# Graph-network kernel on one core: the order of work in the first batch element, and which queue loads the biases

## The chip, the cores and the metric

The kernel runs on one core of a Trainium2 chip. A core has TensorE (PE in the profile, with its weight loads as PEld), VectorE (DVE), ScalarE (ACT), GpSimd (POOL) and SyncE (SP); DMAs are issued here by SP and by POOL. The metric is the device time of one execution in microseconds (us); less is better. The time of the kernel before is a median of 3 runs.

## The reference, cut to what matters

There are 16 batch elements of 1024 nodes with 128 features, each with a dense 1024x1024 adjacency matrix `adj`, all in float32. A first graph layer and then a network of four layers are applied, each followed by a residual and a layer norm:

```python
degree = adj.sum(-1)
sum_neighbors = einsum('bid,bij->bjd', x, adj) / degree
x = layernorm(x + relu(concat([x, sum_neighbors]) @ W.T + b))

# four times, on fpass = x, later on concatenations with earlier layers' features
src_agg = einsum('bjv,bij->biv', nodes @ ws + bs, adj / row_norms)
dst_agg = einsum('bjv,bji->biv', nodes @ wd + bd, adj / column_norms)
fpass = tanh(concat([src_agg, nodes @ wn + bn, dst_agg]) @ wu + bu)

x = layernorm(x + fpass)
```

The kernel multiplies each layer's `ws`, `wd`, `wn` by the parts of `wu` beforehand ("folding"), and the row and column norms are sums of squares of `adj`, raised to the power -0.5.

## The kernel before, in words

The 16 elements go one after the other. While element b runs its four layers, element b + 1 is loaded and its first layer, norms and factors are prepared in the shadow of b's matmuls. Element 0 has nobody ahead of it, so lines 1131 to 1461 are an order written out by hand: each line of Python puts one instruction at the end of one engine's queue, and an engine works through its queue in order. "Hooks" hang work of the other engines at a numbered step of a layer's matmuls. Only this opening, and helpers it calls, are touched.

- **Loads.** `adj[0]` comes as four pairs of row blocks (`load_pair`, L1138), each pair half by SP and half by POOL. Block i = h*4 + k; the pairs come in the order 4-5, 6-7, 0-1, 2-3. After the pairs SP issues the broadcast bias `b0r` (L1198), the weights of layers 0 and 1 (L1200), two of the eight DMAs of row quarter 2, the nine small bias rows of set 0 (`load_biases`, L1163), the rest of row quarter 2, then bias set 1, layer 2's weights, bias set 2, layer 3's weights, and the row quarters 3, 0 and 1 (`load_rows`, L669). The row quarters are a second copy of `adj[0]`, read row-wise, which is scaled by ACT (`scale_rows`, L684) and transposed by DVE (`transpose_rows`, L690) into `at`.
- **First layer.** PE accumulates `x` times each block into `pa` (`gather`, L1242), two halves per block. `to_xT` (L1179) transposes x, `into_rows("px", ...)` (L1264) multiplies it by half of W, `gathered` (L1271) copies `pa` out, `into_rows("pg", ...)` multiplies that by the other half. DVE adds the bias (`x_and_bias`, L1274), the second product (`with_degrees`, L1277), the residual (`with_x`, L1283) and takes the norm's statistics (`two_stats`, L1287), whose powers POOL computes (L1301, L1303); `written` (L1305) writes the normed rows, one of them by ACT with `norm_write_act`. `to_x1` (L1310) transposes them for layer 0's messages.
- **Squares.** ACT squares each block; POOL sums the squares into `sq[4]` (`add_square`, L1232), while DVE adds `sq[7]` to `sq[6]` (L1322), `sq[2]` to `sq[1]` (L1341, names `first` = 2, `second` = 3) and finally `sq[3]` to the sum (L1404). `root_inverses` (L395) gives the row factors by a power on POOL; `inverses` (L382) does the same for the columns from PE's `pc`.
- **Folding.** `bias_columns` (L1169) transposes a set of biases on PE; `fold_begin` (L200) and `fold_end` (L224) make the folded weights of a layer on PE and copy them out on ACT. `fold_end` of layer 2 does its two chunks together, after `to_x1(0)` (L1407).
- **Layer 0 of element 0** (`plain_layer`, L889): 34 steps of one matmul each (two passes in the profile): 2 of own weights (`z`), 8 and 8 of `d` on the unscaled `a`, 16 of `z` on `at`. Its hooks are at L1456: `weights0` (sums of layer 2's weights, nine DVE instructions) at step 0, the column `inverses` at 2, the transposes of row quarters 2 and 3 at 3, `cinv0` (column factors into a row, PE and ACT) at 6, scaling of quarter 0 at 8, `second0` at 11 (DVE multiplies four tiles by `cinv`), `fold_last` at 13 (layer 3's folding, then scaling of quarter 1), four such multiplications on POOL at 14 (L1459), and so on. `finish(0)` after the last step and ACT's tanh (L1107) release the last messages of layer 1.

Of the kernel before, what the change touches and what calls it, by code (L numbers as in the profile page):

```python
# [23 lines left out]
def adj_resnorm_kernel(ctx: ExitStack, tc: tile.TileContext, x, adj, w0, b0, layers, out):  # L24
# [33 lines left out]
    nc = tc.nc  # L58
# [162 lines left out]

        return biases if later else biases()

    def fold_end(l, fetched):  # L224
        _, wur, _, wm, wTs = fetched
        for c in range(CHUNKS[l]):
            pm = small(f"wm{l}_{c}", [HW]) if c < 2 else product(f"wm{l}_{c}")
            for k in range(3):
                nc.tensor.matmul(pm[:, k * P:(k + 1) * P], wTs[c][:, k], wur[:, PART[k]],
                                 start=True, stop=True)  # L230
            nc.scalar.copy(message_weights_of(wm, l, c), pm[:, :2 * P].rearrange("p (a v c) -> p a v c", a=2, v=2))
            nc.scalar.copy(own_weights(wm, l, c), pm[:, 2 * P:3 * P])
        if l not in PAIRED:
            nc.sync.dma_start(wsave[l], wm.rearrange("p c v -> p (c v)")[:, :WIDTH[l]])
        elif l == 3:
            nc.sync.dma_start(wsave[l], wm)
# [923 lines left out]
    columns = [raw.take(len(v)) for v in biases_of]  # L1160
    bcs = [columns[0][:, 1:5], columns[0][:, 5:], columns[1], columns[2]]

    def load_biases(i, q):  # L1163
        for k, v in enumerate(biases_of[i]):
            q.dma_start(in_rows[k:k + 1, i * P:(i + 1) * P], v.rearrange("(o p) -> o p", o=1))

    b0r = one.tile([P, N], F32, tag="acc", name="b0r")[:, :P]
# [28 lines left out]
    places[1] = one.tile([P, 2 * NJ, HW // 2], F32, tag="T2", name="rows1_0")  # L1196
    rows, fetched = {}, []
    nc.sync.dma_start(b0r, b0.rearrange("(o p) -> o p", o=1).to_broadcast([P, P]))  # L1198
    for l in (0, 1):
        fetched.append(fetch_weights(raw, l, nc.sync, bcs[l], None if l else wm))  # L1200
    load_rows_piece(0, 2, places[2], 0, QB, (0,))
    load_biases(0, nc.sync)
    rows[2] = [load_rows_piece(0, 2, places[2], 0, QB, (1, 2, 3))]
    for l in (2, 3):
        load_biases(l - 1, nc.sync)
        fetched.append(fetch_weights(raw, l, nc.sync, bcs[l]))
    wm = as_chunks(wm, 0)
    for q in (3, 0, 1):
        rows[q] = load_rows(0, q, [places[q]])

    nc.vector.memset(mhalf, -0.5)
# [20 lines left out]
    def add_square(i):  # L1232
        nc.gpsimd.tensor_add(sq[4], sq[4], sq[i])
# [8 lines left out]
    def gather(h, i):  # L1242
        nc.tensor.matmul(pa[h], xn[:, i], a[:, i, half(h)], start=(i == BPH), stop=(i == BPH - 1))
# [3 lines left out]
            square(i)  # L1247
            degree(i)

    def gathers_of(h, k):  # L1250
        for i in range(h * BPH + k, h * BPH + k + 2):
            for h2 in (1, 0):
                gather(h2, i)

    agT = one.tile([P, N], F32, tag="f1T", name="agT0")
    xw = one.tile([P, NB, D], F32, tag="f23T", name="xw0")
# [60 lines left out]
    squares_of(*PAIRS[0])  # L1317
    gathers_of(*PAIRS[0])
    squares_of(*PAIRS[1])
    gathers_of(*PAIRS[1])  # L1320
    to_xT(0)
    nc.vector.tensor_add(sq[6], sq[6], sq[7])  # L1322
    add_square(5)
    add_square(6)
    degree_inverses(1)
    squares_of(*PAIRS[2])
    gathers_of(*PAIRS[2])
    add_square(0)
    first, second = 2, 3
    nc.scalar.activation(sq[second], a[:, second, :], AF.Copy, accum_out=cols[:, 2 * NB + second:2 * NB + second + 1])  # L1330
    degree(first)
# [2 lines left out]
    square(first)  # L1334
    degree_inverses(0)
    x_and_bias(1)
    gathered(1)
    into_rows("px", xT, 0, 0)
    into_rows("pg", agT, 1, 1)
    square(second)  # L1340
    nc.vector.tensor_add(sq[1], sq[1], sq[first])  # L1341
    add_square(1)
    x_and_bias(0)
    gather(0, first)
    bias_columns(0)
    gather(0, second)
    gathered(0)
# [4 lines left out]
    into_rows("pg", agT, 1, 0)  # L1352
    two_stats(1, 2)
    root_inverses(cols, inv, slice(NB))
    biases()
    fold_end(0, fetched[0])
    with_degrees(0, range(2))
    written(1, 0, norm_write_act)
    biases = fold_begin(1, fetched[1], later=True)
    for q in range(1, BPH):  # L1360
        written(1, q)
    with_degrees(0, range(2, BPH))
    spread = row_inverses(0, inv)
    to_x1(1)
    biases()
# [1 line left out]
    with_x(0)  # L1367
    two_stats(0, 0)
    two_stats(0, 2)
    for q in range(BPH):  # L1370
        written(0, q)

# [11 lines left out]
    for b in range(B):  # L1384
# [7 lines left out]
        f1 = feature(b, "f1T")  # L1392
        if b == 0:
            def row_factors0():
                scale_rows(rows[2], 2, rinv, range(2, QB))
                scale_rows(rows[3], 3, rinv)

            def second_x1():
                nonlocal rinv
                bias_columns(1)  # L1400
                fold_begin(2, fetched[2])
                rinv = gather_inverses(0, spread)
                scale_rows(rows[2], 2, rinv, range(2))
                nc.vector.tensor_add(sq[4], sq[4], sq[second])  # L1404
                ahead["tr"] = column_transpose(0, st0)

            def factors_and_fold():  # L1407
                to_x1(0)
                fold_end(2, fetched[2])
                column_reduce(0, st0, ahead["tr"])  # L1410

            ahead = {}
            t = messages(b, 0, feats, wm, {0: second_x1, 1: factors_and_fold, 2: row_factors0}, with_sums=False)
            cinv = {}

            def columns0(rows, h, engine=nc.vector):
                scale_columns(a, cinv[0], rows, half(h), engine)

            def weights0(destination, finish):
                sums_of_weights(2, fetched[2][3])  # L1420
                weight_sums(own_seven(2, fetched[2][3]))
                nc.sync.dma_start(wsave[2], fetched[2][3])

            def rows0(destination, finish):
                for q in (2, 3):
                    transpose_rows(rows[q], q, at)

            def cinv0(destination, finish):
                cinv[0] = factor_rows_now(0, 1, inv, "cinv")

            def second0(destination, finish):
                columns0(range(NJ, NB), 1)
                destination(1, cinv[0])

            def first_rows(destination, finish):
                for q in (0, 1):
                    transpose_rows(rows[q], q, at)
                columns0(range(NJ), 1)

            def fold_last(destination, finish):  # L1440
                bias_columns(2)
                fold_begin(3, fetched[3])
                scale_rows(rows[1], 1, rinv)

            def first0(destination, finish):
                destination(0, cinv[0])
                columns0(range(NJ), 0)

            def sums0(destination, finish):
                combine_1(y)  # L1450
                combine(2, y, T)
                finish(1)
                combine_1(yt)
                combine(3, y, T)

            hooks = {0: weights0, 2: lambda *_: inverses(0, st0, NB), 3: rows0, 6: cinv0,  # L1456
                     8: lambda *_: scale_rows(rows[0], 0, rinv), 
                     11: second0, 13: fold_last, 15: first_rows, 16: lambda *_: fold_end(3, fetched[3]),
                     14: lambda *_: columns0(range(NJ, NB), 0, nc.gpsimd), 18: first0, 26: sums0}  # L1459
            T = combined(0, "T")  # L1460
            plain_layer(b, 0, feats, t, wm, a, at, f1, "acc", hooks)
            wm = message_weights(b, 1)
            a2 = load(n)
            xs2 = load_spread(n)
        else:
            w = {}
            if nxt:
                st = begin_sums(n)
            t = messages(b, 0, feats, wm)
            if nxt:  # L1470
                w["a"] = load(n)
            Q = combined(b, "Q")
            ahead = {}

            def weights1(ahead=ahead):
                combine(4, y, T)
                ahead["wm"] = message_weights(b, 1)

            def rows3():
                transpose_rows(rows[0], 0, at)  # L1480

            def sums1(w=w, st=st):
                if nxt:
                    for i in range(2):
                        squares_of_row(n, w["a"], st, i)

            def additions(*which, then=(), w=w, st=st):
                def issue():
                    if nxt:
                        for i in which:  # L1490
                            add_squares(n, st, i)
                        for i in then:
                            squares_of_row(n, w["a"], st, i)
                return issue

            hooks = {0: rows3, 3: weights1, 5: lambda: combine_1(yt), 7: lambda: combine(2, yt, Q),
                     9: lambda: combine(3, yt, Q), 15: sums1, 16: additions(1), 17: lambda: combine(4, yt, Q),
                     18: additions(then=(2, 3)), 23: additions(2), 27: additions(3)}
            aggregate(b, 0, feats, t, wm, a, at, T, Q, f1, "row", hooks)
            wm = ahead["wm"]  # L1500
            a2, xs2 = w.get("a"), None
# [343 lines left out]
```

## Time and profile before

| | |
|---|---|
| median of 3 runs | 2378.79 us (2378.77 to 2379.21) |
| the profiled execution | 2379.08 us |
| its span, first to last instruction | 2377.3 us, so 1.8 us lie around it |
| PE busy | 2364.5 us, 99% |
| DVE busy | 2094.0 us, 88% |
| ACT busy | 980.7 us, 41% |
| POOL busy | 274.1 us, 12% |
| granted TensorE clock, mean | 0.998 |

One execution is shown. In a timeline row the columns are start and duration in us, engine, line and operation, out<-in with the shapes, how many were merged, and in brackets the idle time before it and what ended that. A line such as L249 is that of a helper and serves several layers. A row with xN runs from the first one's start to the last one's end. Time in this text counts from the span's start.

### The profile page before, as it was taken

How to read it: one execution, taken by the hardware profiler on the slowest of the kernel's cores; microseconds unless marked ns; L12 is line 12 of the kernel's file. 1: busy time of each engine (PE TensorE's matmuls, PEld its weight loads, DVE VectorE, ACT ScalarE, POOL GpSimd, SP SyncE). 2: the span in 40 equal slices, each digit the busy share in tenths (PEclk: the TensorE clock that was granted, in tenths of full speed). 3: DMA queues.
4: the chain of work that ended last, by engine and by line, in shares of the span. 5: the costliest groups of instructions: out<-in, count | busy, mean ns of one | idle time of the engine just before them, and what ended most of it. 6: DMA issues, size and time to landing. Idle time of an engine off the chain costs nothing.

```text
span 2377.3 us, 39282 instructions
## 1 busy us (share of the span) xinstructions
PE 2364.5 (99%) x15268; PEld 1323.0 (56%) x15268; DVE 2094.0 (88%) x2835; ACT 980.7 (41%) x1858; POOL 274.1 (12%) x102
## 2 busy tenths in 40 slices
PE   8999999999999999999999999999999999999998
PEld 5455555555555555555655555555555555555555
DVE  7999998998989989889988889898899998998954
ACT  5425334352443524445243452534425334352322
POOL 4000111101111011110011110111100111101100
PEclk9999999999999999999999999999999999999999
DMA  9537263362634527244273442635436263362400
GB/s 208 126 87 148 58 136 76 79 142 49 153 66 95 119 52 168 51 104 108 63 156 68 98 97 72 151 67 119 84 76 146 58 139 75 80 140 49 100 22 22
DMA packets 363548, 232.10 MB, mean 98 GB/s; under 512 B 150385, under 2 KB 334466, under 8 KB 363362
## 3 DMA queue, kind: packets, MB, share of 16 engines
q1 hardware_dynamic: 360722, 226.24, 42.9%
q0 software_dynamic: 816, 2.49, 0.4%
q8 instruction: 121, 1.98, 0.4%
q10 hardware_dynamic: 1824, 0.85, 0.1%
q14 instruction: 65, 0.53, 0.1%
HBM read 209.66 MB, written 19.84 MB: 97 GB/s over the span
## 4 chain that ended last, share of the span: by engine, by line
PE 96%; DMA 2%; DVE 1%; SPq 0%; ACT 0%; issue 0%; POOLq 0%; POOL 0%; DVEq 0%
PE m L1094 43%; PE z L1094 26%; PE pt L249 9%; PE pt_z L249 5%; PE m_f L624 5%; PE z_f L624 3%; PE pw L249 2%; PE m3s L1094 2%; DMA Q<-in_adj_dram 1%; PE pt_p L249 1%; DMA b0r<-in_L_gnn_b_dram 1%; SPq L681 0%; DMA a<-in_adj_dram 0%; DVE a L436 0%; DMA wsave<-wm 0%
## 5 line engine op out<-in xcount | busy, mean ns | idle before, releaser
L1094 PE MATMUL m<-a,t 128*64 128x512 f32 x1008 | 426.8, 593 | 0.0
L1094 PE MATMUL m<-at,t 128*64 128x512 f32 x1008 | 420.4, 592 | 0.0
L1094 PE MATMUL m<-T,S 128*64 128x512 f32 (+1 forms) x1040 | 398.6, 572 | 0.0
L1094 PE MATMUL m<-Q,S 128*64 128x512 f32 x880 | 392.3, 592 | 0.0
L484 POOL TENSOR_TENSOR rs<-ve,mhalf 128x32 f32<-128x32 f32 x30 | 191.6, 6387 | 1019.3 <-DVE ve L482 1019.3
L1094 PE MATMUL z<-at,t 128*64 128x512 f32 (+1 forms) x520 | 229.6, 579 | 0.0
L1094 PE MATMUL z<-a,S 128*64 128x512 f32 x504 | 228.3, 592 | 0.0
L1094 PE MATMUL z<-Q,t 128*64 128x512 f32 (+1 forms) x520 | 227.5, 580 | 0.0
L1094 PE MATMUL z<-a,t 128*64 128x512 f32 (+1 forms) x520 | 227.4, 580 | 0.0
L1094 PE MATMUL z<-at,S 128*64 128x512 f32 x504 | 226.6, 592 | 0.0
L1094 PEld LDWEIGHTS m<-Q,S 128*64 128x64 f32 x880 | 119.4, 137 | 185.1 <-issue 184.8
L1094 PEld LDWEIGHTS m<-T,S 128*64 128x64 f32 x1040 | 133.4, 137 | 122.6 <-issue 117.5
L1094 PEld LDWEIGHTS m<-at,t 128*64 128x64 f32 x1008 | 133.6, 137 | 113.7 <-issue 113.7
L1094 PEld LDWEIGHTS m<-a,t 128*64 128x64 f32 x1008 | 131.5, 137 | 97.5 <-issue 92.8
L946 ACT COPY e<-m 64x512 f32<-64x512 f32 x63 | 36.6, 582 | 338.9 <-PE m L1094 338.5
L1094 PE MATMUL z<-T,t 128*64 128x512 f32 (+2 forms) x400 | 173.0, 575 | 0.0
L397 POOL TENSOR_TENSOR inv<-cols,mhalf 128x16 f32<-128x16 f32 (+1 forms) x16 | 49.6, 3102 | 937.7 <-DVE cols L396 937.7
L436 DVE TENSOR_TENSOR a<-a,cinv 128x512 f32<-128x512 f32 x252 | 153.1, 681 | 0.0
L324 ACT ACTIVATE sq<-a 128x1024 f32<-128x1024 f32 x120 | 125.8, 1050 | 32.7 <-DVE acc L331 18.8
L1094 PEld LDWEIGHTS z<-Q,t 128*64 128x64 f32 x520 | 69.6, 137 | 106.0 <-issue 105.7
L249 PEld LDWEIGHTS pt<-wm,f1T 128*64 128x64 f32 x1536 | 112.0, 137 | 26.7 <-issue 14.7
L319 ACT ACTIVATE a<-a 128x1024 f32<-128x1024 f32 x120 | 125.3, 1045 | 0.4
(329 smaller groups left out, 4997.6 us busy)
## 6 DMA issues: line engine op xcount, KB each, us to landing
a<-in_adj_dram SPq DMA_DIRECT2D x120, 512.0 KB
rows<-in_adj_dram SPq DMA_DIRECT2D x480, 64.0 KB
a<-in_adj_dram SPq DMA_DIRECT2D x240, 128.0 KB
wm<-wsave SPq DMA_DIRECT2D x32, 704.0 KB
wm<-wsave SPq DMA_DIRECT2D x31, 320.0 KB
xs<-in_x_dram SPq DMA_DIRECT2D x60, 128.0 KB
cinv<-dr SPq DMA_DIRECT2D x30, 256.0 KB
dinv<-dr SPq DMA_DIRECT2D x30, 256.0 KB
```

The source lines that it names most:

```text
L249: nc.tensor.matmul(out[s], x[:, s], y, start=start, stop=stop)
L319: nc.scalar.activation(a[:, i, :], a[:, i, :], AF.Copy, accum_out=degree)
L324: nc.scalar.activation(sq, a[:, i, :], AF.Square, accum_out=state["cols"][:, i:i + 1])
L397: nc.gpsimd.tensor_tensor(inv[:, s], cols[:, s], mhalf[:, s], ALU.pow)
L436: engine.tensor_mul(a[:, i, s], a[:, i, s], cinv[:, s])
L484: nc.gpsimd.tensor_tensor(rstd, ve, mhalf[:, :n], ALU.pow)
L624: nc.tensor.matmul(o, x_, y_, start=start, stop=stop)
L946: nc.scalar.copy(e0[high], A[high])
L1094: nc.tensor.matmul(o, x, y_, start=start, stop=stop)
```

## The change

It reorders the opening and moves some DMAs. SP loads five of the nine biases of set 0 straight after `b0r`, then the weights of layers 0, 1 and 2, then row quarters 2, 3 and 0, then layer 3's weights, then quarter 1. POOL's queue loads the other biases between its additions of squares. `to_xT(0)` goes between the two gathers of the second pair, and x's products `px` of half 0 before the third pair. `gather(0, first)` goes ahead of `pg` of half 1. The DVE addition of `sq[2]` to `sq[1]` is dropped: POOL adds `sq[1]` and, after `root_inverses`, `sq[2]` by itself. Row 0 of half 1 is written by ACT ahead of layer 0's folding copies. `fold_end` of layer 2 is split around `to_x1(0)`. All eight rows of quarter 2 are scaled in one place. The column inverses come at step 4, the weight sums at 5, the transposes at 6, `cinv0` at 8, and quarter 0's scaling at 9.

```diff
-    def fold_end(l, fetched):
+    def fold_end(l, fetched, chunks=None):
         _, wur, _, wm, wTs = fetched
-        for c in range(CHUNKS[l]):
+        for c in range(CHUNKS[l]) if chunks is None else chunks:
...
-    def load_biases(i, q):
-        for k, v in enumerate(biases_of[i]):
+    def load_biases(i, q, s=slice(None)):
+        for k, v in list(enumerate(biases_of[i]))[s]:
...
-    for l in (0, 1):
+    load_biases(0, nc.sync, slice(0, 5))
+    for l in (0, 1, 2):
         fetched.append(fetch_weights(raw, l, nc.sync, bcs[l], None if l else wm))
-    load_rows_piece(0, 2, places[2], 0, QB, (0,))
-    load_biases(0, nc.sync)
-    rows[2] = [load_rows_piece(0, 2, places[2], 0, QB, (1, 2, 3))]
-    for l in (2, 3):
-        load_biases(l - 1, nc.sync)
-        fetched.append(fetch_weights(raw, l, nc.sync, bcs[l]))
     wm = as_chunks(wm, 0)
-    for q in (3, 0, 1):
+    for q in (2, 3, 0, 1):
+        if q == 1:
+            fetched.append(fetch_weights(raw, 3, nc.sync, bcs[3]))
         rows[q] = load_rows(0, q, [places[q]])
...
-    def gathers_of(h, k):
+    def gathers_of(h, k, between=None):
         for i in range(h * BPH + k, h * BPH + k + 2):
             for h2 in (1, 0):
                 gather(h2, i)
+            if between is not None and i == h * BPH + k:
+                between()
...
-    gathers_of(*PAIRS[1])
-    to_xT(0)
+    gathers_of(*PAIRS[1], lambda: to_xT(0))
     nc.vector.tensor_add(sq[6], sq[6], sq[7])
     add_square(5)
+    load_biases(0, nc.gpsimd, slice(5, 7))
     add_square(6)
+    load_biases(0, nc.gpsimd, slice(7, 8))
     degree_inverses(1)
+    into_rows("px", xT, 0, 0)
     squares_of(*PAIRS[2])
     gathers_of(*PAIRS[2])
     add_square(0)
+    load_biases(0, nc.gpsimd, slice(8, 9))
+    add_square(1)
+    load_biases(1, nc.gpsimd)
...
     x_and_bias(1)
+    x_and_bias(0)
     gathered(1)
-    into_rows("px", xT, 0, 0)
+    gather(0, first)
     into_rows("pg", agT, 1, 1)
     square(second)
-    nc.vector.tensor_add(sq[1], sq[1], sq[first])
-    add_square(1)
-    x_and_bias(0)
-    gather(0, first)
     bias_columns(0)
     gather(0, second)
...
     root_inverses(cols, inv, slice(NB))
+    add_square(first)
     biases()
+    written(1, 0, norm_write_act)
     fold_end(0, fetched[0])
-    with_degrees(0, range(2))
-    written(1, 0, norm_write_act)
     biases = fold_begin(1, fetched[1], later=True)
     for q in range(1, BPH):
         written(1, q)
-    with_degrees(0, range(2, BPH))
+    with_degrees(0, range(BPH))
...
     two_stats(0, 2)
+    load_biases(2, nc.gpsimd)
...
-                scale_rows(rows[2], 2, rinv, range(2, QB))
+                scale_rows(rows[2], 2, rinv)
...
-                scale_rows(rows[2], 2, rinv, range(2))
...
             def factors_and_fold():
+                fold_end(2, fetched[2], (0,))
                 to_x1(0)
-                fold_end(2, fetched[2])
+                fold_end(2, fetched[2], (1,))
...
-            hooks = {0: weights0, 2: lambda *_: inverses(0, st0, NB), 3: rows0, 6: cinv0,
-                     8: lambda *_: scale_rows(rows[0], 0, rinv), 
+            hooks = {4: lambda *_: inverses(0, st0, NB), 5: weights0, 6: rows0, 8: cinv0,
+                     9: lambda *_: scale_rows(rows[0], 0, rinv), 
```

## The prediction

> **What bounds the kernel now.** I read the waits of PE first, then PE's, DVE's and POOL's timelines up to 90 us. PE is busy 99% of the span. These are all of its waits:
>
> ```profile
> PE pa L1243 <- DMA a<-in_adj_dram: 2.0, 1, 2.0
> PE idle L1187 <- DVE mhalf L1211: 1.5, 1, 1.5
> PE biases L1172 <- DMA biases<-in_L_gnn_bu_dram: 0.8, 1, 0.8
> PE px L1269 <- ACT w0T L1192: 0.7, 1, 0.7
> PE bm L211 <- DMA raw<-in_L_gnn_wu_dram: 0.7, 1, 0.7
> PE pt L249 <- ACT f1T L1107: 0.6, 1, 0.6
> PE on L1762 <- DVE f23T L1757: 0.3, 1, 0.3
> PE bm L211 <- ACT wm L232: 0.3, 1, 0.3
> ```
>
> After 80.61 us (the wait for f1T) PE never waits again until 2365 us. So the change moves the end by as much as it moves PE at 80.61. Its matmuls stay the same, so it can win only the waits from 19.6 us on: 0.76 + 0.30 + 0.69 + 0.58 = 2.3 us, 0.1%. It can lose more.
>
> **Part 1: x's products and the biases, on PE.** One gather pass takes 0.428 us (8 in 3.43). Before, the second pair ends at 18.99, the transposes fill the time to 19.59, and the third pair starts at 19.67: the "wait" there is 0.08 us. After, the transposes go at 17.28 (four passes earlier), the pair ends at 19.42, px (0.89 us, 24.90 to 25.79) runs to 20.31, and the third pair starts 0.64 later. Then px is missing, which gives back 0.89, but gather(0, first) (0.86) is put ahead of pg: pg of half 1 starts at 25.79 + 0.64 - 0.89 + 0.86 = 26.4, about 0.55 later than before. The bias transpose comes at 27.59 + 0.64 - 0.89 = 27.3 instead of 28.52, if the biases are there, and the second gather ends 1.2 us earlier.
>
> Are they? SP's issues of weights at 10.24, 12.13, 14.18, 15.58, 17.11, 18.71 and 20.75 each start when the DMA eight places ahead has landed. Five biases take five of these places, so layer 0's weights go out from 18.71 to some 23.5; they are needed at 28.4. POOL's DMAs cost it 0.53 us each (row of its loads of a), and the ninth bias goes out at 23.7 to 24.2. A POOL DMA took 3.2 us to land in the emptiest stretch (w0n): 26.9. I cost it at nothing; 1 us late would still be covered by the 1.5 us of part 2. Layer 2's weights come before the row quarters, so the 0.69 us goes as well. The last quarter landed at 57.9; DMA had nearly idle slices at 26 to 28 (2 GB/s) and 32 to 38 us, so it comes sooner, and its scaling waits for PE anyway (part 5). If it landed after 59, that would cost one for one.
>
> **Part 2: row 0 ahead of the fold's copies, on ACT.** pg is 0.55 late, but with_x(1) no longer overlaps POOL (0.95 becomes 0.69), so the statistics are 0.25 late, shift is there at 31.5 instead of 31.27, and ACT writes row 0 at 31.6 (0.40). Only then come the two copies (L231, L232: 0.27 and 0.27 between starts, 0.27 to finish) that free PE's bank: 32.6. PE, ready at 31.25, starts bm there, against 32.96. Of the 1.2 us won, 0.2 to 0.4 is left.
>
> **Part 3: the addition of sq[2] on POOL.** This is the step I weigh most. These are POOL's and DVE's rows:
>
> ```profile
> 14.80 2.38 POOL L1233 TENSOR_TENSOR sq<-sq,sq 128x1024 f32<-128x1024 f32 x1
> ...
> 26.15 2.35 POOL L1233 TENSOR_TENSOR sq<-sq,sq 128x1024 f32<-128x1024 f32 x1 [2.38 <-DVE sq L1341]
> ...
> 32.04 1.64 POOL L397 TENSOR_TENSOR inv<-cols,mhalf 128x8 f32<-128x8 f32 x1
> 54.59 1.63 POOL L436 TENSOR_TENSOR a<-a,cinv 128x512 f32<-128x512 f32 x1 [5.68 <-PE d L913]
> ```
>
> ```profile
> 16.54 1.72 DVE L1322 TENSOR_TENSOR sq<-sq,sq_row 128x1024 f32<-128x1024 f32 x1
> 24.78 1.22 DVE L1341 TENSOR_TENSOR sq<-sq,sq 128x1024 f32<-128x1024 f32 x1
> 28.09 0.95 DVE L1285 SCALAR_TENSOR_TENSOR x1n<-xw,xn 128x512 f32<-128x512 f32 x1
> 33.93 0.69 DVE L1285 SCALAR_TENSOR_TENSOR x1n<-xw,xn 128x512 f32<-128x512 f32 x1
> 54.40 0.68 DVE L436 TENSOR_TENSOR a<-a,cinv 128x512 f32<-128x512 f32 x1
> ```
>
> A DVE instruction with two SBUF inputs stands still while a POOL addition runs: L1322 overlaps it by 0.64 and takes 0.50 longer than L1341; L1285 overlaps by 0.41 and takes 0.26 longer than without. In turn POOL's L436 overlaps a DVE product by 0.49 and takes 0.36 longer than its median of 1.27. Each time the loss is the overlap less 0.14.
>
> [...] The adds here agree to 0.14 us; POOL's powers do not (a DVE L719 of 2.29 us inside a power of 7.41 us at 173.8 takes no longer). [...]
>
> The dropped DVE addition (1.22) frees time in which DVE would wait for pg, so it gains nothing. The new POOL addition follows the power directly: from 32.04 + 0.2 + 1.64 = 33.9 to 36.25. DVE then wants L403 and with_x(0), both with two SBUF inputs, at 34.0 instead of 33.71. Blocked, with_x(0) starts at 36.3, and `written(0, 3)` ends at 40.5 instead of 38.2. Queued behind it on DVE are the first message addition, rinv and the sum of squares; PE waits for the rows.
>
> **Part 4: layer 2's fold around x1's transposes.** Twelve passes take 1.34. The products of x1 (half 0) start at 41.55 now. Unblocked, six passes go ahead, the transposes run at 39.1, and the products start near 40.4: 1.15 won. Blocked, PE waits until 40.6, then for rinv, which lies on DVE behind the first message addition and frees a PSUM bank for the second chunk: 41.5, plus 0.67: the products start at 42.2, 0.6 lost.
>
> **Part 5: column factors at step 4.** From there PE runs without a break: products 1.95, own weights 1.75, then two steps (1.71) ahead of `pc`: at 47.6. DVE waits for `pc` with the weight sums (2.3) behind it: 0.25 + 0.65 + 2.3 + 4.65 (transposes of two quarters) until `second0`'s four products, 7.8 after `pc`. POOL's four products are released 7.3 after it (six steps, `cinv0` 0.89, one more step). In the profile DVE's began at 52.62 and POOL's at 54.59, nearly apart; now they meet. POOL's effective start at 54.95 is where the DVE product's reading ends, before the next DVE start at 55.00. So I take them to alternate: POOL's first from 47.6 + 7.3 = 54.9, then four turns of 1.27 - 0.14 (POOL) and 0.60 (DVE), 6.9 us, to 61.9 instead of the 57.9 that DVE would reach alone. With 0.6 (destination) and 2.35 (quarter 0) the transposes of quarter 1 start at 64.9, against 61.79: +3.1. If DVE keeps its turn (lower end of this cost: nothing), the start is set by ACT's scaling, which waits for PE at step 13: 61.77 + 0.6 = 62.4. From that row to 79.12 DVE has no wait, so the message that PE awaits moves by as much. PE itself is done 0.6 late, so its wait grows from 0.58 to 3.1.
>
> **Sum.** +3.1 by DVE; where a turn meets no wait (the fourth may), up to 0.5 less: I take +2.9. On the profiled execution's 2379.08 that is 2382.0; its time stands 0.29 above the median, so 2381.7 for the median. The forecast lies within 0.2% (4.8 us) of the median, about what a measurement of this kernel can tell from no change; the cases below are taken from the median of 2378.79.
>
> **Rivals.**
> - The adds do not collide (DVE slips in, or the power ends later): part 4's 1.15 is won on PE, DVE's products stay unhindered. 2377.6. Against it: two overlaps above, both blocked. Chance 0.13.
> - Blocked at with_x(0), but DVE keeps its turn in `second0`: +0.6, 2379.4. For it: nothing here shows alternation, only that POOL comes in as a DVE read ends. Chance 0.24.
> - Slower still, by the clock. These windows of 3.41 us show the rule, columns as in the windows view (PE busy first, granted clock behind POOL):
>
> ```profile
> 8.03:11.44 3.41, 1.45 (x7) 0.81 (x6) 1.10 (x1) 1.12 (x3) 0.79 (x2) 1.00 1.06 306
> 11.44:14.86 3.42, 3.42 (x6) 1.37 (x5) 1.83 (x3) 1.67 (x4) 1.17 (x4) 0.50 1.04 244
> 79.71:83.12 3.41, 2.83 (x24) 1.49 (x22) 2.50 (x5) 3.29 (x6) 0.00 (x0) 1.00 1.05 203
> ```
>
>  A window with 43% PE work was followed by one at half clock, one with 83% was not. With 2.9 us of waiting, the window around 81 us can fall to 15%; the next then loses 3.41 / 2 = 1.7: 2383.4. A wait of 1.9 near 39 us could do it a second time: 2385.1, slower by over 0.2%. It decides from a bound between 43% and 83%, and by where the windows lie. Chance 0.27, of which 0.10 for twice.
> - The change does not do what it says, because POOL's biases or layer 0's weights land after 30 us: PE waits as before or longer, +2 to +6. Chance 0.05.
>
> The forecast itself has 0.31. The range takes in all but the tail of the first rival below 2377.4 and the second clock loss: 2377.4 to 2383.7. Faster by over 0.2% (2374.0) needs more than PE's waits hold: 0.01. Slower by over 0.2% (2383.55): 0.10 for the clock twice, 0.03 for an upper part of it once, 0.02 for late loads: 0.15. Same: 0.84.
>
> **What would show it.** PE's waits without L1172 and the 0.69; `bm` near 32.7; a POOL L1233 at about 33.9 and DVE's L1285 at its end; then L436 on DVE and POOL in turns near 56 to 62 us; the wait for f1T at some 3 us; the granted clock around 83 us. It is wrong if L1285 runs 0.69 inside POOL's addition, or if L436 on DVE stays four in 2.45.

## The result and the profile after

The changed kernel takes 2384.04 us (median of 15 runs, 2382.11 to 2385.96), the kernel before 2378.79 us (15 runs, 2377.58 to 2379.99): a ratio of 1.0023, 95% interval [1.0015, 1.0031]. It is slower by 5.3 us where 2.9 were forecast, 0.34 us above the top of the range. The runs also lie wider apart than before: 3.9 us from the fastest to the slowest, against 2.4.

The profiled execution of the changed kernel took 2385.48 us (span 2383.4). All of PE's waits in it, with the line, what it waited for, and total, times and longest in us:

```profile
PE pt L249 <- ACT f1T L1107: 2.6, 1, 2.6
PE idle L1187 <- DVE mhalf L1208: 1.5, 1, 1.5
PE pa L1240 <- DMA a<-in_adj_dram: 1.0, 2, 0.8
PE bm L211 <- ACT wm L232: 1.0, 1, 1.0
PE px L1268 <- ACT w0T L1192: 0.7, 1, 0.7
PE x1tr L1312 <- DVE x1n L525: 0.7, 2, 0.4
PE on L1764 <- DVE f23T L1759: 0.4, 1, 0.4
PE wm L229 <- DVE rinv L412: 0.4, 1, 0.4
PE wm L229 <- DVE e L904: 0.2, 1, 0.2
```

The waits for the biases and for layer two's weights are gone, as meant. In their place stand waits for x1's rows, for rinv and for `e`, 1.0 instead of 0.3 us for layer 0's copies, and 2.6 instead of 0.6 us for f1T. POOL's timeline of this kernel shows the two places that the forecast named:

```profile
31.48 1.64 POOL L397 TENSOR_TENSOR inv<-cols,mhalf 128x8 f32<-128x8 f32 x1
33.09 2.35 POOL L1230 TENSOR_TENSOR sq<-sq 128x1024 f32<-128x1024 f32 x1
...
56.01 6.31 POOL L436 TENSOR_TENSOR a<-a,cinv 128x512 f32<-128x512 f32 x4 [4.79 <-PE d L913]
```

And DVE's, at the same times:

```profile
33.15 2.34 DVE L403 TENSOR_TENSOR sp<-inv,group 128x32 f32<-128x32 f32 x1
35.41 0.68 DVE L1284 SCALAR_TENSOR_TENSOR x1n<-xw,xn 128x512 f32<-128x512 f32 x1
...
56.30 6.57 DVE L436 TENSOR_TENSOR a<-a,cinv 128x512 f32<-128x512 f32 x4
```

L403 is an instruction of 0.19 us. It comes 0.06 us after POOL's addition and stands for as long as that runs; with_x(0) follows at its end. Later the four products on each engine go in turns: 6.57 us on DVE, where before they took 2.45, and 6.31 on POOL. Both were forecast (6.9 us for the second).

What was forecast only as a rival is in the windows of the clock. Columns as in the prediction: stretch, length, then PE busy first, and behind POOL the granted clock:

```profile
37.97:41.38 3.41, 2.36 (x15) 1.44 (x15) 3.05 (x9) 1.13 (x3) 2.73 (x6) 1.00 1.22 199
41.38:44.79 3.41, 3.41 (x16) 1.59 (x16) 3.38 (x5) 3.39 (x10) 0.00 (x0) 0.50 1.23 194
82.34:85.75 3.41, 1.30 (x12) 0.92 (x14) 2.67 (x5) 2.08 (x4) 0.00 (x0) 1.00 1.03 203
85.75:89.16 3.41, 3.41 (x12) 1.22 (x10) 2.67 (x5) 3.41 (x7) 0.00 (x0) 0.50 1.05 210
```

Two windows in which PE waited are each followed by one at half clock (0.50) with PE busy throughout, 1.7 us lost each time, half of 3.41.

**Where the time is.** Executions differ by up to 2 us in the opening (PE waits 0.5 us for the rows of a in e1 and 2.6 in e2, and the clock's first full window starts at 7.41 and 5.65): mark A below lies at 24.61 us in e1 and at 26.66 in e2. So spans of single profiles must not be compared. I cut PE's timeline at three marks instead: A, the first product of `pg` half 1; B, the first L913 product; C, the first message product behind the wait for f1T. From C to PE's last product only element 0's rest and the other elements run.

| kernel | A to B | B to C | C to the last | windows at half clock after A and before the end |
|---|---|---|---|---|
| before | 17.64 | 37.18 | 2290.85 | none |
| changed | 19.50 | 39.59 | 2292.95 | two |
| changed, two fills (e5) | 17.84 | 39.59 | 2291.28 | none |

A to C grew by 4.27 us, C to the end by 2.10. The opening gave 0.44 back (A at 25.35 instead of 25.79), so the two profiles differ by 5.93 us on PE. Mark A has one drawback: the change puts `gather(0, first)` (0.86 us) and the place of `px` ahead of it, so that PE takes 10.96 us from its ninth gather to A instead of 10.23. Some 0.7 us of what A to B gains against the kernel before is paid there.

### The profile page after: what moved, and what is told of

The parts are those of the page before. It is cut to its first block, busy times and chain, and to the rows that moved or that the text cites. A ratio compares the mean times of both kernels' runs of the same rounds, so it can differ in the third digit from the quotient of the medians.

```text
span 2383.4 us, 39291 instructions
## 1 busy us (share of the span) xinstructions
PE 2369.0 (99%) x15268; PEld 1448.9 (61%) x15268; DVE 2098.3 (88%) x2834; ACT 980.4 (41%) x1858; POOL 283.2 (12%) x115
## 4 chain that ended last, share of the span: by engine, by line
PE 96%; DMA 2%; DVE 1%; SPq 0%; issue 0%; ACT 0%; POOLq 0%; POOL 0%; DVEq 0%
PE m L1094 39%; PE z L1094 30%; PE pt L249 9%; PE pt_z L249 5%; PE m_f L624 5%; PE z_f L624 3%; PE pw L249 2%; PE m3s L1094 2%; DMA Q<-in_adj_dram 1%; PE pt_p L249 1%; DMA b0r<-in_L_gnn_b_dram 1%; DVE a L436 0%; DMA rows<-in_adj_dram 0%; DMA a<-in_adj_dram 0%; DMA raw<-in_L_gnn_ws_dram 0%; DVE at L696 0%
## 5 line engine op out<-in xcount | busy, mean ns | idle before, releaser
L436 DVE TENSOR_TENSOR a<-a,cinv 128x512 f32<-128x512 f32 x252 | 157.2, 698 | 0.0
L249 PE MATMUL pt<-wm,f1T 128*64 128x128 f32 (+1 forms) x1536 | 127.7, 309 | 2.6 <-ACT f1T L1107 2.6
```

The lines of the kernel that those rows point to most:

```text
L249: nc.tensor.matmul(out[s], x[:, s], y, start=start, stop=stop)
L436: engine.tensor_mul(a[:, i, s], a[:, i, s], cinv[:, s])
```

## The experiments

All diffs are against the changed kernel unless another is named. The theory: three losses add up, POOL's addition stopping DVE (A to B), the turns in second0 (B to C), and windows at half clock that PE's new waits bring. Rivals: the new queue of the loads costs (A); the order of the hooks costs by itself (B); the clock's phase alone makes the difference (C).

### e1_add_back: the addition of sq[2] back on DVE

```
     load_biases(0, nc.gpsimd, slice(8, 9))
-    add_square(1)
...
     square(second)
+    nc.vector.tensor_add(sq[1], sq[1], sq[first])
+    add_square(1)
...
-    add_square(first)
```

> Undoes only part 3: sq[2] is added by DVE again, right after square(3), with POOL's addition of row 1 behind it. Theory (three losses that add up: POOL's addition stops with_x(0) for 2.2 us; DVE and POOL take turns in second0, 4.1 us on DVE; PE's two waits that follow each can cost a window at half clock, 1.7 us): with_x(0) falls from 0.69+2.15 of standing to 0.7, the products of x1 half 0 start about 1.0 us earlier than after's 41.29, the turns in second0 stay (6.3 to 6.6 us for DVE's four), the wait for f1T stays above 2 us; time 2381 to 2382.5, that is 1.5 to 3 us under the changed kernel's 2384.04. Rival A (the queue of loads): no different from the changed kernel, 2383.5 to 2384.5. Rival B (only the order of the hooks costs, POOL's addition nothing): 2383.5 to 2384.5 too.

Measured: 2380.64 us, ratio to before 1.0009 [1.0000, 1.0018]. DVE's L403 takes 0.19 and with_x(0) 0.69 us; A to B falls to 16.30. The turns stay (6.57 us), and so does the wait for f1T, 2.6 us. Rivals A and B expected 2383.5 or more and fall. The gain over the changed kernel is 3.4 us: 1.5 between A and B beside the clock (17.84 in e5, 16.30 here), 0.4 by a pause told under e11; what is left, 1.5, I put down to fewer windows at half clock, which the profiles allow (none here, two there) but medians alone can't show. The granted clock of the single executions points the same way: it is 0.998 in eight of the changed kernel's 15 and in one of these 11.

### e2_hooks_back: the dictionary of hooks as before

```
-            hooks = {4: lambda *_: inverses(0, st0, NB), 5: weights0, 6: rows0, 8: cinv0,
-                     9: lambda *_: scale_rows(rows[0], 0, rinv), 
+            hooks = {0: weights0, 2: lambda *_: inverses(0, st0, NB), 3: rows0, 6: cinv0,
+                     8: lambda *_: scale_rows(rows[0], 0, rinv), 
```

> Undoes only part 5: the dictionary of hooks is the one of before (weight sums at step 0, inverses at step 2, and so on). Theory: DVE's four products of second0 run in about 2.5 us again without POOL beside them, the wait for f1T falls to 1 us or less; with_x(0) still stands 2.15 us; 2379.5 to 2381.5, the upper end if the window behind 41 us still falls to half clock. Rival A (loads): 2383.5 to 2384.5. Rival C (the clock's phase alone makes the 5 us): 2383 or more.

Measured: 2381.55 us, 1.0011 [1.0002, 1.0020]; L436 takes 2.45 us on DVE, the wait for f1T 0.6. L403 still stands 2.15 us. It is 0.05 us above the top of what was expected: B to C is 38.71, not 37.18, for a reason that e3 shows more plainly.

### e3_both_back: both undone, the rest of the change kept

> Undoes parts 3 and 5, keeps the rest (x's products in the wait, row 0 before the copies, layer two's fold around the transposes, the loads on two queues). Theory: no long wait is left, 2376.8 to 2378.5, so 0.3 to 2 us under the kernel before. Rival A (loads cost): 2381 or more. If the two parts add up, the two single gains over the changed kernel sum to this one's within 1.5 us (the windows of the clock do not add).

Measured: 2379.32 us, 1.0002 [0.9993, 1.0010]. No gain was left, which I had not expected. A to B is 16.41, 1.23 us better than before, of which 0.7 is paid ahead of A: from the ninth gather to B it is 27.39 us instead of 27.87. The early products of x, the split folding and the loads earn 0.5 us there. But PE's timeline shows where it goes:

```profile
44.02 3.70 PE L913 MATMUL d<-a,t 128*128 128x512 f32 x8
48.96 1.09 PE L361 MATMUL cinvp<-ident,inv 128*128 128x128 f32 x8 [1.24 <-POOL inv L397]
```

With the old hooks DVE does the weight sums ahead of the inverses. PE, now earlier, meets `cinvp` before POOL's power is done, and waits 1.24 us, more than it had won. So the new order of the hooks is what the earlier PE needs; it fails by what it makes meet. Rival A (2381 or more) falls for good. The two single gains, 3.4 and 2.5, sum to 5.9, this one's is 4.7: within the 1.5 us that was said.

### e4_fill_f1T and e5_fill_two: work for PE in the wait for f1T

```
+        def fill():
+            pd = small(f"fill{b}", [HW])
+            for i in range(5):
+                nc.tensor.matmul(pd, ident, f1[:, half(1)], start=True, stop=True)
...
-        t = messages(b, 1, feats, wm)
+        t = messages(b, 1, feats, wm, {1: fill} if b == 0 else {})
```

(e5 has `range(2)`.) Both add products that nobody reads.

> The changed kernel with five extra products of 128x512 whose result nobody reads, on PE ahead of the wait for f1T in element 0 (0.43 us each, 2.1 of the 2.6 us of waiting), so that PE is busy there without doing more of the work. Theory (the wait costs a second time through the clock): the window behind 85.7 us is granted full speed, 2382.0 to 2382.8, 1.2 to 2.0 us under the changed kernel, with DVE's and POOL's rows as they were. Rival (the wait costs itself alone): the same as the changed kernel, 2383.7 to 2384.4.

> The changed kernel with two instead of five extra products ahead of the wait for f1T. In the run with five, each came out as two passes of 0.43 us on PE, ten in all, 4.56 us, so that PE was late for the real products by 1.8 us; what was won by the clock went there. Two are four passes, 1.7 of the 2.6 us. Theory (the wait costs a second time, through a window at half clock): 2382.2 to 2382.9, up to 1.8 us under the changed kernel, message products still at about 84.4 us. Rival (the wait costs itself alone): 2383.7 to 2384.4.

Measured: with five 2384.17 us, 1.0023 [1.0015, 1.0032]; with two 2382.24 us, 1.0015 [1.0006, 1.0023]. The first was mis-sized by me: each product came out as two passes, ten in 4.56 us, so the real products began at 86.27 instead of 84.44. Yet its profile shows the half clock at 41.54 only, and from C to the last product 2291.27 instead of 2292.95: what the late start cost, 1.8, the clock gave back. With two, PE's timeline reads

```profile
77.60 1.95 PE L249 MATMUL pt<-wm,f1T 128*64 128x256 f32 x16
79.47 1.98 PE L1511 MATMUL fill<-f1T,ident 128*128 128x512 f32 x4
82.14 1.95 PE L249 MATMUL pt<-wm,f1T 128*64 128x256 f32 x16 [0.68 <-ACT f1T L1107]
```

DVE and POOL are as in the changed kernel, B to C is the same 39.59 us, PE does more work, and the kernel is 1.8 us faster. None of e5's 11 executions has a granted clock of 0.998. That shows that the wait for f1T costs a second time through the clock. Rival C falls in part: the phase decides whether, the wait decides that there is something to decide.

### e6_apart: the transposes of quarter 3 behind second0

```
             def rows0(destination, finish):
-                for q in (2, 3):
-                    transpose_rows(rows[q], q, at)
+                transpose_rows(rows[2], 2, at)
...
             def second0(destination, finish):
                 columns0(range(NJ, NB), 1)
                 destination(1, cinv[0])
+                transpose_rows(rows[3], 3, at)
```

> The changed kernel, with one move: the two transposes of row quarter 3 go on DVE behind second0 instead of ahead of it, so that DVE's four products start about 2.3 us sooner and are through before POOL's four begin. Nothing else moves; the hooks keep their order. Theory (it is the two engines meeting that costs 4 us): L436 on DVE falls from 6.57 to 2.5 to 3.3 us, quarter 1's transposes start where ACT's scaling ends, near 63.3 instead of 65.7, no wait for f1T is left, 2379.7 to 2381.3. Rival B (the order of the hooks costs by itself, weight sums and inverses late): 2383 or more.

Measured: 2379.73 us, 1.0005 [0.9996, 1.0014]; 4.3 us less than the changed kernel, by one move on DVE. DVE's timeline:

```profile
53.41 2.45 DVE L436 TENSOR_TENSOR a<-a,cinv 128x512 f32<-128x512 f32 x4
55.78 0.69 DVE L904 TENSOR_TENSOR e<-d,cinv 128x512 f32<-128x512 f32 x1
56.39 4.61 DVE L696 STREAM_TRANSPOSE at<-Q 128x1024 f32<-128x1024 f32 x4
62.58 2.37 DVE L696 STREAM_TRANSPOSE at<-rows 128x1024 f32<-128x1024 f32 x2 [1.58 <-ACT rows L688]
```

POOL's four run from 55.36 to 61.13, beside the transposes, which take 4.61 us as they do alone (4.62 in the changed kernel). B to C is 37.19, that of the kernel before. The order of the hooks costs nothing; the meeting cost all that B to C had grown by (2.40 us of the 4.3). Behind C this profile has no window at half clock, 1.67 us less; in A to B it has none either, which the move on DVE doesn't explain. PE still waits 0.6 us for f1T, where none was expected. Rival B falls.

### e7_add_back_apart: both collisions gone

The edits of e1 and e6 together.

> The same move, and sq[2] is added by DVE as before. Theory: both collisions are gone, with_x(0) does not stand, second0 takes 2.5 to 3.3 us, quarter 1's transposes start at 59.4 instead of 61.8, finish(0) at 76.7, f1T is there before PE asks for it at 77.9; 2376.2 to 2377.5, 1.5 to 2.8 us faster than the kernel before. Rival: DVE has a second bound behind it and finish(0) stays at 79: 2379 or more, as with the two parts undone.

Measured: 2377.94 us, 0.9997 [0.9988, 1.0005], the fastest of all by its median and 1.2 us under the runs of the kernel before beside it (2379.11), which the interval cannot tell from no change. A to B 16.28, B to C 37.18: the gain between A and B now reaches C. PE still waits 0.6 us for f1T, which I had expected to go: quarter 1's transposes started 1.6 us after the quarter before them, waiting for ACT's scaling as in e6, because ACT does the folding's copies first. The median lies between the two expectations.

A third meeting is left, which I had overlooked. With sq[2] back on DVE, POOL's addition of sq[1] comes later and with_x(1) runs into it:

```profile
26.98 2.36 POOL L1230 TENSOR_TENSOR sq<-sq,sq 128x1024 f32<-128x1024 f32 x1 [0.61 <-DVE sq L1345]
```

```profile
28.77 1.11 DVE L1284 SCALAR_TENSOR_TENSOR x1n<-xw,xn 128x512 f32<-128x512 f32 x1
```

with_x(1) takes 1.11 to 1.55 us in all six kernels with DVE's addition (e1, e3, e7 to e10), 0.95 in the kernel before and 0.69 in the seven with POOL's, as the prediction said of these. A to B follows it: less with_x(1) it is 15.15 to 15.17 us in e1, e3, e7 and e8.

### e8_add_back_fill: e1 with two fills

> sq[2] added by DVE as before, hooks of the change, and two extra products ahead of the wait for f1T. Its sister without them has the same span in its profile as the kernel with both parts undone (2377.4 and 2377.3), but a median 1.3 us longer. Theory (in some executions its wait of 2.6 us costs a window at half clock): the span of the profile stays at 2377.4, the median falls from 2380.6 to 2379.0 to 2379.7 and the runs draw together. Rival (the 1.3 us have another cause): 2380.3 or more.

Measured: 2380.13 us, 1.0005 [0.9996, 1.0014]. Half a microsecond under e1, not 1.3: between the two expectations. My reason was wrong. I had compared the spans of e1's and e3's profiles, which agree because e1's opening happened to be short (A at 24.61, against 25.45). From A to C e1 takes 55.90 and e3 55.04 us: the 0.9 us are there, in the turns of second0. And the wait of 2.6 us in e1's profile cost no clock, since a border between windows fell into it:

```profile
75.67:79.08 3.41, 2.25 (x17) 1.06 (x16) 3.41 (x3) 0.00 (x0) 0.00 (x0) 1.00 1.03 208
79.08:82.50 3.42, 1.99 (x18) 1.35 (x20) 2.51 (x5) 2.77 (x6) 0.00 (x0) 1.00 1.04 208
82.50:85.91 3.41, 3.41 (x18) 1.28 (x16) 3.27 (x6) 3.41 (x8) 0.00 (x0) 1.00 1.07 207
```

66% and 58% busy, and full clock behind both.

### e9_rows1_early: e7, and quarter 1 scaled ahead of layer three's folding

```
-                scale_rows(rows[1], 1, rinv)
...
-                     11: second0, 13: fold_last, 15: first_rows, 16: lambda *_: fold_end(3, fetched[3]),
+                     12: lambda *_: scale_rows(rows[1], 1, rinv),
+                     11: second0, 16: fold_last, 15: first_rows, 17: lambda *_: fold_end(3, fetched[3]),
```

> The kernel with both collisions gone, plus one more move: ACT scales row quarter 1 at step 12, ahead of layer three's folding, which goes to steps 16 and 17. In that kernel's profile DVE waited 1.57 us for this scaling and PE 0.58 us for f1T. Theory (DVE's chain to f1T is what set PE, and after the move PE sets itself): quarter 1's transposes start some 1.5 us sooner, the wait for f1T is gone, 2377.0 to 2377.8 with its sister at 2377.9, 1.2 to 2 us under the kernel before. Rival (something else on ACT or in PE's banks comes late in its place): 2378 or more.

Measured: 2381.09 us, 1.0006 [0.9997, 1.0014], in runs from 2377.93 to 2382.97: on the rival's side. The wait for f1T is gone and B to C falls to 36.96, so 0.2 us were to be had. In the profile a window at half clock came after a wait of 1.9 us for `bm`, in the part of the kernel that is the same as in e7:

```profile
29.94:33.35 3.41, 1.54 (x15) 1.30 (x14) 2.64 (x15) 1.30 (x4) 2.56 (x4) 1.00 0.84 200
33.35:36.76 3.41, 3.41 (x17) 2.78 (x19) 3.22 (x14) 1.56 (x5) 1.25 (x2) 0.50 1.23 186
```

Seven of e9's 11 runs are above 2380 us, of e7's one. The longer wait has a cause in this profile: with_x(1) stands behind POOL's addition for longer than in e7 (1.54 us instead of 1.11), and `bm` waits 1.87 instead of 1.44. But the moved step comes more than 20 us later, so why more executions than in e7 should be hit is open; it may be chance.

### e10_copies_first: e7 with part 2 undone

```
-    written(1, 0, norm_write_act)
     fold_end(0, fetched[0])
+    written(1, 0, norm_write_act)
```

> The kernel with both collisions gone, with part 2 undone: the two copies of layer 0's fold go on ACT ahead of row 0 of x1. Theory (rows 1 to 3 come from DVE, and the transposes of x1 wait for them whatever ACT does first): bm's wait of 1.4 us shrinks to 0.3 or less, but a wait of about 1 us for x1's rows appears at the next line; the products of x1 start within 0.3 us of its sister's; 2377.6 to 2378.3. Rival (part 2 has cost the bm wait): 2376.5 to 2377.2.

Measured: 2378.32 us, 0.9997 [0.9987, 1.0006]. The wait for `bm` falls from 1.4 to 0.3 us, and two of 0.3 appear at x1's transposes. A to B is 16.65 against 16.28, which looks like the forecast's 0.2 to 0.4 us for row 0 first. But with_x(1) stood longer in this execution:

```profile
28.04 1.55 DVE L1284 SCALAR_TENSOR_TENSOR x1n<-xw,xn 128x512 f32<-128x512 f32 x1
```

That is 0.44 us more than in e7. A to B less with_x(1) is 15.10 us here and 15.15 to 15.17 in the kernels with row 0 first, so the profiles show no gain of part 2, and the medians (2378.32 and 2377.94) lie too near to each other to show one. The rival, 2376.5 to 2377.2, falls.

### e11_two_memsets: e6 and two small instructions on DVE

```
     square(second)
+    nc.vector.memset(inv[:, 3 * NB:], 0.0)
+    nc.vector.memset(inv[:, 3 * NB:], 0.0)
```

> The changed kernel with the transposes of quarter 3 behind second0 (2379.7), and two small memsets of zeros over zeros on DVE in the place of the addition that the change took from it. All five kernels with POOL's addition of sq[2] show an idle 0.42 us before the same DVE instruction, L815 at 115 to 120 us, that nothing in the trace explains, and none of the five without. Theory (it goes by the number of DVE's instructions ahead of it, as if one came late into its queue): the 0.42 us are gone from L815 or stand before another instruction. Rival (it comes from POOL's addition or its sums): still 0.42 us at L815. Time 2379.2 to 2380 either way.

Measured: 2380.85 us, 1.0005 [0.9996, 1.0014], with four runs at 2378.5 to 2379.3 and six at 2380.7 to 2382.1, so the median, above the 2380 expected, says little. The profile answers: no pause, and C to the last product is 2290.85, as in the kernels without POOL's addition (2290.79 to 2290.85), against 2291.28. The two lines of DVE, first in the changed kernel,

```profile
119.18 0.69 DVE L812 TENSOR_TENSOR t<-t,pt 128x512 f32<-128x512 f32 x1 [0.19 <-PE pt L249]
120.34 0.69 DVE L815 TENSOR_TENSOR t<-t 128x512 f32<-128x512 f32 x1 [0.47 <-DVE t L812]
```

and here:

```profile
113.34 0.69 DVE L812 TENSOR_TENSOR t<-t,pt 128x512 f32<-128x512 f32 x1 [0.18 <-PE pt L249]
114.13 0.69 DVE L815 TENSOR_TENSOR t<-t 128x512 f32<-128x512 f32 x1
```

L815 waits 0.47 us behind L812 there and 0.11 here. So the pause doesn't come from POOL's addition, which this kernel keeps. That it goes by how many instructions DVE has had fits all 14 profiles, but no run varied that number alone; why is open.

### e12_add_later: e6 with POOL's addition after x1's statistics

```
-    add_square(first)
...
     two_stats(0, 2)
+    add_square(first)
     load_biases(2, nc.gpsimd)
```

> The changed kernel with the transposes of quarter 3 behind second0, and POOL's addition of sq[2] put behind the statistics of x1's half 0 instead of right behind the power. POOL still adds, later. Theory (the addition costs by where it meets with_x(0), not by being on POOL): with_x(0) runs 0.69 us without standing, DVE's L1405 waits about 1 us for POOL but DVE has 1.5 us of waiting for pc behind it; products of x1 as early as with DVE's addition, 2377.7 to 2378.7, against 2379.73 with the addition where the change has it. Rival (POOL's addition costs wherever it is): 2379.3 or more.

Measured: 2380.12 us, 1.0005 [0.9996, 1.0014], the rival's side of the line. with_x(0) no longer stands (0.69 us), but POOL's and DVE's timelines show what does:

```profile
36.77 2.35 POOL L1230 TENSOR_TENSOR sq<-sq 128x1024 f32<-128x1024 f32 x1
```

```profile
35.91 0.60 DVE L525 TENSOR_SCALAR x1n<-x1n,mv,rst 128x128 f32<-128x128 f32 x2
36.84 2.62 DVE L525 TENSOR_SCALAR x1n<-x1n,mv,rst 128x128 f32<-128x128 f32 x2 [0.34 <-POOL rst L1300]
```

The next pair of rows, tensor-scalar instructions with one tensor from SBUF, takes 2.62 us instead of 0.60: they stand as well, and A to B is the same 17.82 as with the addition where the change has it. My theory holds in that the addition costs by what it meets, but I had the wrong list of what can be met.

The prediction spoke of two SBUF inputs alone; these rows add a second kind, 2.62 us instead of 0.60. It is not every DVE instruction: e6's transposes, which also have one tensor from SBUF, took 4.61 us beside POOL's products and 4.62 alone.

## Why the prediction was wrong

Its steps in order, with the marks of the table above.

**PE's opening.** Right in kind. From the ninth gather to the seventeenth PE took 4.88 us instead of 4.11 for the products of x (0.64 forecast more, 0.77 measured). The forecast's own sum puts A at 26.4, 0.61 later than before and not its 0.55. A came at 25.35, since in this execution the first gather started sooner (9.92 us instead of 10.35) and the window at half clock of the profile before, 11.44 to 14.86 us, has no counterpart here. The biases were there: no wait for L1172. The loads show no cost (e3, rival A).

**Row 0 ahead of the copies.** `bm` started at 31.62, 6.3 us after A, forecast 6.2. The gain of 0.2 to 0.4 us that the forecast gave to it isn't shown (e10).

**POOL's addition.** Right: L403 stood 2.15 us, forecast some 2.2 together with with_x(0). It follows the power at 33.09, 0.8 earlier than forecast, as A was 1.05 earlier. with_x(1) took 0.69 us, as forecast.

**Layer two's folding.** Unhindered, A to B is 16.3 (e1, e7) instead of 17.64; less the 0.7 paid ahead of A, some 0.6 is won, forecast 1.15. One reason is that with_x(1) stands there. With the addition A to B is 17.83 (e2, e5, e6), 0.2 more than before and with the 0.7 some 0.9 lost, forecast 0.6.

**Column factors.** Right: the turns, 6.57 us against 6.9, and PE's wait for f1T, 2.6 against 3.1. That POOL comes in where a DVE product's reading ends was an estimate of mine; no trace shows where a read ends, only the turns. B to C without any half clock grew by 2.41 us.

**Sum.** It holds within half a microsecond for what it counted. e5 is the changed kernel with its late window of the clock taken away, and at 2382.24 stands 3.1 us above the runs of the kernel before beside it; the sum was +2.9. In the 3.1 is a pause that the sum left out, and that nothing in the trace of before announced: it makes C to the last product 0.43 us longer (2291.28 instead of 2290.85).

**The step that failed is the third rival, "slower still, by the clock": its mechanism was right, its chance and its place were not.** The sum held the clock at nothing. The rival priced it at 1.7 us with a chance of 0.27, laid on the windows of one profile, and the range was cut below the second loss. But the windows keep their own time: in the changed kernel's profile the two at half clock start 10 and 23 times 3.41 us behind the first full one (41.38 and 85.75 behind 7.24). In the 14 profiles of this case the first full window starts anywhere from 4.39 to 7.41 us, 3.02 of a period's 3.41. So I take it that a wait meets them at random, and the chance can be estimated. By the column of PE busy in the windows, those up to 45% busy were followed by half clock (43% in before, 38% in e6, 45% in e9, 38% in the changed kernel); those of long products from 48% up were not (48% in e2, 50% in e8, 58% in e1). So, as an estimate from these windows, an idle share of some 53%, 1.8 us, is needed in one of them. With PE busy on both sides, a wait of 3.1 us misses that only if a border falls into its middle: 1 - (2 x 1.8 - 3.1) / 3.41 = 0.85; one of 2.6 us, 0.71. Even the bound of 43% that the prediction had would have given 0.77. Its own forecast of the wait made the loss the likeliest case: 2381.7 + 1.7 = 2383.4, and a second one, 2385.1, had to be in the range. Measured: e5's 2382.24 without the late window, 2384.04 with it, 1.8 us.

The early window does not fit the column: 69% busy brought half clock in the changed kernel and in e4, while 69% in e6, 70% in e11 and even 59% in e12 (37.20 to 40.62 us) kept full clock. The column overstates isolated short products: two transposes of x1 alone are put down at 0.58 us, four in a row at 0.60. Counted instead by the time from one start to the next in back-to-back rows (0.43 us for a 128x512 pass, 0.11 for a 128x128 one), both kinds of window come into one order. From the first window at full clock on, those with 31% (e6), 33% (e9), 36% (before), 37% and 38% (changed) and 38.8% (e4) were followed by half clock, and those from 39.4% (e1, near its end) and 40% (e6, e11) up were not; e12's, 38.3%, is the only one out of order. So I estimate the bound near 39% by this count, with some 2.1 us idle. The wait for f1T as e1's trace has it, laid at every place of the window, then loses in six of ten, and the early stage as in e5's trace in two of ten. The times don't test this closer: two fills took 1.8 us off the changed kernel, but only 0.5 off e1, whose wait is as long.

**Rivals.** That the adds do not collide, or that DVE keeps its turn, is refuted by the rows above. The late loads did not happen: no wait for L1172.

## What to carry to other kernels

A wait on TensorE had two prices here: its length and, with a chance that I estimate from its length over the 3.41 us of a window, another 1.7 us. Work out that chance instead of reading one profile's windows, whose first full one started at 4.39 to 7.41 us in the 14 profiles. If the wait can't go, two products that nobody reads took the second price away here (2384.04 to 2382.24 us, though only 0.5 us off e1). Before an operation is moved to POOL or two engines' work is brought closer together, list what DVE does in that time: beside POOL's additions and products here, instructions with two SBUF inputs (L403 2.34 us instead of 0.19) and tensor-scalar ones (2.62 instead of 0.60 for a pair) stood, transposes (4.61, alone 4.62) did not. A part that earns its gain can show nothing, as in e3, until the order that it upsets is mended too. And before a difference between two profiles is given to an edit, look whether the same instruction stood longer in one of them, as with_x(1) did in e10.

## What the hardware showed that I had not expected

- DVE's tensor-scalar instructions stood during a POOL addition (2.62 instead of 0.60 us for a pair, e12), not only those with two SBUF inputs.
- Half clock followed windows in which PE was partly busy: by the column 43% in the kernel before and 45% in e9 (36% and 33% from start to start), and up to 39% from start to start (38.8% in e4). The windows are 3.41 us long, and their starts differ from profile to profile (4.39 to 7.41 us for the first full one).
- A longer idle time before one DVE instruction (L815), 0.47 to 0.48 us instead of 0.10 to 0.11, in all six profiles with one DVE addition less and nothing in its place, and in none of the eight others; two memsets took it away (e11).
